# Joining row scans of layer 1 into 256 columns, and preparing two inputs a phase earlier

## The chip, the core and the metric

The kernel runs on one core of a Trainium2 chip. The metric is the time of one execution on the device, in microseconds, as the median of several runs. The engines are TensorE (PE; its weight loads are listed as PEld), VectorE (DVE), ScalarE (ACT), GpSimd (POOL) and SyncE (SP), which does nothing here but issue DMAs. ACT and POOL issue a few DMAs too.

## What is computed

The input `x` has 32 images of 48 channels, 64 rows and 128 columns, in float32. There are two layers. Each normalises its input by groups of channels, passes a convolution along one axis through the image row by row and then column by column, and adds its input:

```python
def step(w, b):
    def f(carry, inp):
        nxt = inp + _conv1d(carry, w, b)      # 48 x 48 channels, 5 taps
        return (nxt, nxt)
    return f
...
_, d_rest = jax.lax.scan(step(down_w, down_b), xs[0], xs[1:])      # 64 rows, downwards
...
_, u_rest = jax.lax.scan(step(down_w, down_b), u0, seq)            # 64 rows, upwards, the same weights
...
_, r_rest = jax.lax.scan(step(right_w, right_b), ws[0], ws[1:])    # 128 columns, to the right
...
_, l_rest = jax.lax.scan(step(left_w, left_b), l0, R[Ww - 2::-1])  # 128 columns, to the left
...
x = x + _L0_conv_ref(_gn(x), ...)
x = x + _L1_conv_ref(_gn(x), ...)
```

Each step of a scan needs the step before it. Different images are independent of each other.

## The kernel before

**Groups and phases.** The 32 images are four groups (0 to 3) of `GB` = 8. A row scan handles one group at a time: one row of one group is 128 columns (16 places along the image's width, beside 8 images) on three tiles of 128 partitions that hold 8 x 48 pairs of place and channel. A column scan handles two groups at a time, a pair. `PHASES` (line 103) lists the order of the work; "rows 1,2" means the row scans of layer 1 for group 2, "cols 0,0" the column scans of layer 0 for pair 0. A row phase is 63 steps down and 63 up, a column phase 127 right and 127 left.

**A step.** `step` (line 881) runs the nine products of `PRODUCTS` into three PSUM tiles of 128 columns, one for each of the three tiles of a row, and as each is complete VectorE adds the bias and the input to it and writes the new row or column into SBUF in place (line 903). Each product is two matmul instructions. Two of the nine have 96 weight columns and 120 moving columns, one has 112 weight columns. The order of the products is such that the first product of the next step needs the tile that was completed first. `row_step` and `col_step` call it; `scans` (line 955) yields all steps of a phase one after the other.

**Memory.** A group's 64 rows lie in two of the three `slot`s of the arena, 32 rows in each (`row_views`, line 688). Even phases use slots 0 and 1, odd phases 2 and 1 (`slots`, line 326). Column phases go through the image's width in four quarters, `quarter(k, j)`, one slot each.

**The order written out by hand.** Time is counted in steps. `at(t, fn)` puts work on an agenda, and before each step everything that is due is emitted (`catch_up`, line 1377). `in_order` (line 292) keeps that order on every engine, so each engine, and SyncE's queue of DMAs with it, takes its work strictly as the agenda lists it; an instruction that has to wait holds up all that stand behind it on its engine. An engine isn't held back to the agenda's time, though: it runs ahead as far as its data lets it.

- `plan_rows` (line 1006) loads a group's rows in blocks of 16 (`move_rows` from layer 0's rearranged input, `take_rows` from layer 1's input), has ACT scale them (`scale_rows`, 24 instructions a block), and stores the rows of the up scan in blocks of 8 (`move_rows` to DRAM, 10 DMAs each). Where a column phase follows directly, the last 8 rows go straight from the row layout into the column layout: `send_row` and `send_rest`, about 47 DMAs on each of the queues of SyncE and ACT.
- `plan_cols` (line 1054) loads the quarters, adds the residual on GpSimd, stores the result, and in layer 0 takes the statistics for layer 1 on VectorE and ACT.
- `plan_input` (line 986) prepares one group of the input in six parts: `take_in` fetches a part into a buffer (`nats`), GpSimd rearranges it (`permute`, 16 copies), four DMAs put it out (`put_out`), and ACT takes its statistics (`take_others`). `spread` then emits the small computation of scale and offset, one piece in each step. Group 1 has four buffers; groups 2 and 3 have one.

Layer 0's statistics of group 2 were prepared in cols 0,0, those of group 3 half in rows 0,2 and half in rows 1,0.

`last` is a buffer for the last row of the down scan, which the last step of the up scan adds.

Of the kernel before, what the change touches and what calls it, by code (L numbers as in the profile page):

```python
# [41 lines left out]
GB = 8  # L42
# [35 lines left out]
def weight_runs():  # L78
# [38 lines left out]


@with_exitstack
def kernel(  # L120
# [567 lines left out]
    def row_views(k):  # L688
        return [slot[i].rearrange("p (o h n) -> p o h n", o=NG, h=HALF) for i in slots(k)]

    def row(k, h):
        return row_views(k)[h // HALF][:, :, h % HALF]

    def move_rows(k, h0, h1, to_dram, q=None):

        _, layer, g = PHASES[k]
        view = row_views(k)[h0 // HALF]
        t = (ups if to_dram else source)[layer][g]
        for h in range(h0, h1, E8):
            end = min(h1, h + E8)  # L700
            for o in range(NG):
                for e, c0, c1, p0 in pieces(o):
                    here = view[p0 : p0 + c1 - c0, o, h % HALF : h % HALF + end - h]
# [12 lines left out]

    def take_rows(k, h0, h1, o):

        _, layer, g = PHASES[k]
        view = row_views(k)[h0 // HALF]  # L720
        for e, c0, c1, p0 in pieces(o):
            here = view[p0 : p0 + c1 - c0, o, h0 % HALF : h0 % HALF + h1 - h0]
            for q in range(NQ):
                dma(
                    here[:, :, q * RUN : (q + 1) * RUN],
                    by_quarter(source[layer][g], e, h0, h1, q)[c0:c1],
                )

    def scale_rows(k, h0, h1, groups=range(NG)):
        _, layer, g = PHASES[k]  # L730
        scale, offset = coeffs[layer, g]
        view = row_views(k)[h0 // HALF][:, :, h0 % HALF : h0 % HALF + h1 - h0]
        view = view.rearrange("p o h (k b) -> p o b h k", b=GB)
        for o in groups:
            for b in range(GB):
                args = view[:, o, b], scale[:, o, b : b + 1], offset[:, o, b : b + 1]
                nc.scalar.activation(  # L737
                    args[0], args[0], AF.Identity, bias=args[2], scale=args[1]
                )

    def scale_at_once(k, h0, h1, eng, o0=0, o1=NG):

        _, layer, g = PHASES[k]
        view = row_views(k)[h0 // HALF][:, o0:o1, h0 % HALF : h0 % HALF + h1 - h0]
        view = view.rearrange("p o h (k b) -> p o (h k) b", b=GB)
        for t, op in zip(coeffs[layer, g], (ALU.mult, ALU.add)):
            t = t[:, o0:o1].unsqueeze(2).to_broadcast([FULL, o1 - o0, (h1 - h0) * NK, GB])
            eng.tensor_tensor(view, view, t, op)
# [132 lines left out]
    def step(key, weights, b_at, src, inp, dst, whole, part):  # L881


        ps = [
            ps_step.tile([FULL, N], F32, tag=f"step{o}", name=f"step{o}_{key}")
            for o in range(NG)
        ]
        left = [sum(1 for p in PRODUCTS if p[1] == o) for o in range(NG)]
        seen = [0] * NG
        for i, o, s in PRODUCTS:  # L890
            seen[o] += 1
            m = COLUMNS.get((i, o, s), FULL)
            at = FULL * (o - NG * s - i + 1)
            nc.tensor.matmul(  # L894
                part(whole(ps[o])[0:m], -s),
                weights[:, i, at : at + m],
                part(src(i), s),
                start=seen[o] == 1,
                stop=seen[o] == left[o],
            )  # L900
            if seen[o] == left[o]:
                layer, way = b_at
                nc.vector.scalar_tensor_tensor(  # L903
                    dst(o),
                    whole(ps[o]),
                    bd[:, o, layer, way : way + 1],
                    inp(o),
                    ALU.add,
                    ALU.add,
                )  # L910

    def row_step(k, h, prev, inp, name):
        _, layer, g = PHASES[k]

        def part(t, s):
            return t[:, max(0, s) * GB : N + min(0, s) * GB]

        step(
            f"{layer}{g}{name}{h}",
            wt[f"down{layer}"],  # L920
            (layer, DOWN),
            lambda i: prev[:, i],
            lambda o: inp[:, o],
            lambda o: row(k, h)[:, o],
            lambda ps: ps,
            part,
        )

    def col_step(k, way, v0, v1):
# [10 lines left out]
        def part(t, s):  # L940
# [7 lines left out]
            col(v0),  # L948
            col(v1),
            col(v1),  # L950
            lambda ps: ps.rearrange("p (m b) -> p m b", b=GB),
            part,
        )

    def scans(k):
        if PHASES[k][0] == "rows":
            for h in range(1, H):
                yield lambda h=h: row_step(k, h, row(k, h - 1), row(k, h), "d")
            end = last.rearrange("p (o n) -> p o n", o=NG)
            for h in range(H - 2, -1, -1):  # L960
                yield lambda h=h: row_step(
                    k, h, row(k, h + 1), row(k, h - 1) if h else end, "u"
                )
        else:
            for v in range(1, W):
                yield lambda v=v: col_step(k, RIGHT, v - 1, v)
            for v in range(W - 2, -1, -1):
                yield lambda v=v: col_step(k, LEFT, v + 1, v)


    agenda = []
# [14 lines left out]
    def plan_input(g, times, work, lag, nats, perms):  # L986
# [5 lines left out]
        for j, t in enumerate(times):  # L992
# [11 lines left out]
        spread(t + work + lag + (0, 2, 32, 5)[g], scaling(f"x{g}", 0, g, stats, x_masks, (0, 0, 8, 0)[g]), 1)  # L1004

    def plan_rows(k, t0, prev):
        if k == 1:
# [5 lines left out]
        if k:  # L1013
            for i in range(4):
                if PHASES[k][1]:
                    for o in range(NG):
# [8 lines left out]
        seam = following and follows(k + 1)  # L1025
        if seam:
            cuts = cuts[2:]
            end = t0 + 2 * (H - 1)
# [4 lines left out]
            for q in range(1, NQ):  # L1033
                at(end + 0.1 if q == 1 else end + 1.6, move_rows, k, 0, 2 * E8, True, q)
        for h0, h1 in zip(cuts, cuts[1:]):
            t = t0 + 2 * (H - 1) - h0
            if k == 0:
                t += 16 if h0 >= HALF else 68
            elif not following:
                t = t0 + 92 + 5 * (H - h1) / E8 + (34 if h1 <= HALF else 0)  # L1040
            at(t, move_rows, k, h0, h1, True)
        at(
            t0 + H - 1,
            nc.gpsimd.tensor_copy,
            last.rearrange("p (o n) -> p o n", o=NG),
            row(k, H - 1),
# [7 lines left out]
    def plan_cols(k, t0, prev):  # L1054
# [5 lines left out]
        for i in range(n):  # L1060
# [3 lines left out]
                at(t0 - 13 + i, load_unit, k, 0, i, 2, 4, 0, E8, other)  # L1064
                at(t0 - 6 + i / n, load_unit, k, 0, i, 1, 2, 0, E8, other)
            else:
                early = 30 if after else 46 if k == 2 else 70
# [17 lines left out]
        for n_done, j in enumerate((3, 2, 1, 0)):  # L1085
            first, every = left + 34 + 32 * n_done, 4.5
            if j == 0 and PHASES[k + 1 if not final else k][0] == "rows":
                first, every = (end + 29, 6) if pair else (first, 7)
            units += [(first + every * i, j, i) for i in range(n)]
        stats = None  # L1090
        if layer == 0:
# [62 lines left out]
            store_result(k, 0, i, perm)  # L1154


    starts = [0]
    for kind, *_ in PHASES:
        starts.append(starts[-1] + 2 * ((H if kind == "rows" else W) - 1))
# [24 lines left out]
    at(starts[7] + 50, more_weights, "right", 1, RIGHT)  # L1184
    at(starts[7] + 54, more_weights, "left", 1, LEFT)


    def first_group():
# [191 lines left out]
            in_order(fn, *args)  # L1380

    for k in range(len(PHASES)):
        for one in scans(k):
            catch_up(done)
            in_order(one)
            done += 1
    catch_up(float("inf"))


# [51 lines left out]
```

## Time and profile before

| What | Value |
|---|---|
| Timed, median of 3 | 4165.44 us (4165.31 to 4170.69) |
| Profiled execution, its span from first to last instruction | 4158.1 us (the page gives no other time of it) |
| Mean granted TensorE clock | 0.989 |
| First step of the first scan | 60.7 us |
| DMA | 681.08 MB, mean 164 GB/s; 2008656 of 2208479 packets under 512 B |

The page lists for each engine the busy time, its share of the span and its instructions, then the span in 40 equal slices, the DMA queues, and the costliest groups of instructions. A group's row reads: line, engine, operation, what it writes and reads, shape, count, then busy time in us and mean of one in ns, then the idle time before it and what ended that. A row of stretches reads: the stretch, its length, for each engine its busy time and count of instructions, the granted clock, the DMA engines' share and GB/s. A row of the timeline reads: start, length, engine, line, operation, and in brackets the idle time before it and its releaser. SPq is SyncE's queue: each row there is a run of DMAs as they were issued, not as they landed.

The tiles of a step are named by layer and group or pair and direction: `step_01u` is rows 0,1 upwards, `step_00r` is cols 0,0 to the right. The scans of the phases start at (first matmul, us): rows 0,1 at 323.12, cols 0,0 at 577.40, rows 0,2 at 1081.07, rows 1,0 at 1344.66, rows 0,3 at 1596.38, cols 0,1 at 1850.34, rows 1,1 at 2351.51, rows 1,2 at 2608.13, rows 1,3 at 2857.88, cols 1,0 at 3107.59, cols 1,1 at 3604.21; the last matmul starts at 4101.85.

### The profile page before, as it was taken

The numbers are of one execution on the slowest core, as the hardware profiler recorded it, in microseconds if no ns is written. First come the engines' busy times: TensorE is split into PE (matmuls) and PEld (weight loads), VectorE is DVE, ScalarE is ACT, GpSimd is POOL, SyncE is SP. The second block draws the span as 40 slices with busy tenths as digits, with TensorE's granted clock in tenths as the row PEclk, the third lists the DMA queues.
The fourth block names the chain that finished last, engine by engine and source line by source line (L and its number), as shares of the span: only waits on it lengthen the run. The fifth ranks groups of instructions, "written<-read, shape, count | busy, mean of one in ns | idle before, by whom it ended". The sixth has DMA issues, their size and how long they took to land. (4 is left out here: it accounts for less than half of the span.)

```text
span 4158.1 us, 90227 instructions
## 1 busy us (share of the span) xinstructions
PE 4049.2 (97%) x36724; PEld 4031.7 (97%) x36724; DVE 2141.6 (52%) x6503; ACT 1251.6 (30%) x2440; POOL 826.1 (20%) x763
## 2 busy tenths in 40 slices
PE   6999999999999999999999999999999999999994
PEld 5999999999999999999999999999999999999994
DVE  6454444456654454444457664444444444444444
ACT  4645000536964543000006863423000002200122
POOL 5630010334222000010013220000000015610353
PEclk9999999999999999999999999999999999999997
DMA  9987769669979999258419979959289029999799
GB/s 299 229 184 121 116 127 214 209 159 252 218 188 163 173 163 156 35 103 194 107 30 273 181 147 145 141 93 150 49 141 208 1 55 247 295 257 155 146 233 197
DMA packets 2208479, 681.08 MB, mean 164 GB/s; under 512 B 2008656, under 2 KB 2157376, under 8 KB 2183488
## 3 DMA queue, kind: packets, MB, share of 16 engines
q1 hardware_dynamic: 2063936, 582.35, 68.4%
q10 hardware_dynamic: 141568, 87.46, 8.8%
q0 software_dynamic: 2560, 5.51, 0.5%
q8 instruction: 289, 4.73, 0.5%
q14 instruction: 126, 1.03, 0.1%
HBM read 398.29 MB, written 295.14 MB: 167 GB/s over the span
## 5 line engine op out<-in xcount | busy, mean ns | idle before, releaser
L829 POOL TENSOR_TENSOR arena<-arena 128x2048 f32<-128x2048 f32 x80 | 362.7, 4545 | 1481.7 <-PE step_10l L894 458.3
L737 ACT ACTIVATE arena<-arena,offset,scale 128x256 f32<-128x256 f32 (+2 forms) x744 | 538.4, 818 | 384.4 <-DMA arena<-mid 206.1
L674 POOL COPY arena<-arena 128x256 f32<-128x256 f32 x340 | 201.0, 659 | 447.6 <-DMA arena<-in_x 418.2
L612 ACT ACTIVATE early<-arena 128x256 f32<-128x256 f32 x192 | 129.7, 675 | 443.0 <-DMA arena<-xin 308.1
L894 PE MATMUL step_00r<-arena,early 128*128 128x128 f32 x2286 | 252.1, 274 | 6.1 <-DMA arena<-arena 5.1
L894 PEld LDWEIGHTS step_00r<-arena,early 128*128 128x128 f32 x2286 | 251.2, 185 | 7.0 <-issue 5.5
L894 PE MATMUL step_01r<-arena,early 128*128 128x128 f32 x2286 | 252.2, 274 | 5.8 <-DMA arena<-arena 4.9
L894 PEld LDWEIGHTS step_01r<-arena,early 128*128 128x128 f32 x2286 | 251.3, 185 | 6.6 <-issue 5.3
L894 PE MATMUL step_11r<-arena,early 128*128 128x128 f32 x2286 | 249.3, 272 | 0.3 <-DVE arena L903 0.3
L894 PEld LDWEIGHTS step_11r<-arena,early 128*128 128x128 f32 x2286 | 248.7, 184 | 0.8 <-DVE arena L903 0.7
L894 PE MATMUL step_00l<-arena,wleft 128*128 128x128 f32 x2286 | 249.2, 272 | 0.0
L894 PEld LDWEIGHTS step_00l<-arena,wleft 128*128 128x128 f32 x2286 | 248.7, 184 | 0.0
L894 PE MATMUL step_10l<-arena,wleft 128*128 128x128 f32 x2286 | 248.5, 272 | 0.0
L894 PE MATMUL step_11l<-arena,wleft 128*128 128x128 f32 x2286 | 248.5, 272 | 0.0
L894 PE MATMUL step_10r<-arena,early 128*128 128x128 f32 x2286 | 248.4, 272 | 0.0
L894 PE MATMUL step_01l<-arena,wleft 128*128 128x128 f32 x2286 | 248.4, 272 | 0.0
L894 PEld LDWEIGHTS step_10l<-arena,wleft 128*128 128x128 f32 x2286 | 248.4, 184 | 0.0
L894 PEld LDWEIGHTS step_11l<-arena,wleft 128*128 128x128 f32 x2286 | 248.4, 184 | 0.0
L894 PEld LDWEIGHTS step_01l<-arena,wleft 128*128 128x128 f32 x2286 | 248.4, 184 | 0.0
L894 PEld LDWEIGHTS step_10r<-arena,early 128*128 128x128 f32 x2286 | 248.4, 184 | 0.0
L297 ACT COPY early<-arena 128x1 f32<-128x1 f32 x2 | 0.4, 192 | 709.9 <-DVE arena L903 709.9
L851 ACT COPY arena<-arena 128x256 f32<-128x256 f32 x172 | 99.6, 656 | 362.4 <-POOL arena L829 256.3
(202 smaller groups left out, 7088.5 us busy)
## 6 DMA issues: line engine op xcount, KB each, us to landing
xin<-arena SPq DMA_DIRECT2D x94, 512.0 KB, 4.3
arena<-in_x SPq DMA_DIRECT2D x18, 2048.0 KB, 11.4
arena<-xin SPq DMA_DIRECT2D x96, 384.0 KB, 10.9
arena<-mid SPq DMA_DIRECT2D x384, 96.0 KB, 3.1
upb<-arena SPq DMA_DIRECT2D x192, 192.0 KB, 3.9
arena<-upb SPq DMA_DIRECT2D x96, 384.0 KB, 11.8
arena<-xin SPq DMA_DIRECT2D x174, 192.0 KB, 4.3
mid<-arena SPq DMA_DIRECT2D x32, 1024.0 KB, 11.2
```

The lines of the kernel that those rows point to most:

```text
L297: fn(*args)
L612: nc.scalar.activation(junk[:, 0:n], view[:, b], AF.Identity, accum_out=self.sum[:, i, j : j + 1])
L674: copy(dst[:, r, q], src[:, r0 + r, q])
L737: nc.scalar.activation(args[0], args[0], AF.Identity, bias=args[2], scale=args[1])
L829: eng.tensor_tensor(unit, unit, nat, ALU.add)
L851: copy(by_w(perm)[:, a], src[:, a])
L894: nc.tensor.matmul(part(whole(ps[o])[0:m], -s), weights[:, i, at : at + m], part(src(i), s), start=seen[o] == 1, stop=seen[o] == left[o],)
```

## The change

1. **Order.** "rows 1,0" moves behind "cols 0,1", so that all four row phases of layer 1 stand together.
2. **Joined scans.** Phases 8 and 9 (rows 1,2 and rows 1,3) are `JOINED`: the down scan of each runs together with the up scan of the group before it. `two_row_step` runs one step of both groups as 256 columns, with the same weights, into PSUM tiles of twice the width; VectorE's add covers both halves in one instruction, except in the last step, where it takes two.
3. **Places.** Since a joined group's rows come in while those of the group before go out, in the same slot, rows are loaded in blocks of 8 into the place of the block that has just been stored. `place` and `rows_at` work out where; `plan_rows` loads each block 34 steps ahead and scales it 17 steps ahead, counted in old steps, two for each joined one.
4. **Inputs.** Input 3 of 4 (group 2) is prepared in rows 0,1 instead of cols 0,0, one part each 9.5 steps instead of 13.5; input 4 (group 3) in cols 0,0 at the times that input 3 had.
5. **Small moves.** The residuals of the last quarter of cols 0,0 come later (from `end + 29`, every 6 steps, as those of cols 0,1 do already); the weights for layer 1's columns and the loads of cols 1,0 are moved with the phases.

```diff
@@ PHASES
     ("rows", 0, 2),
-    ("rows", 1, 0),
     ("rows", 0, 3),
     ("cols", 0, 1),
+    ("rows", 1, 0),
     ("rows", 1, 1),
...
+JOINED = (8, 9)
...
+    def place(k, h):
+        first = k
+        while first in JOINED:
+            first -= 1
+        since = k - first
+        turned = (since + 1) // 2 % 2 if h < HALF else since % 2
+        c = h % HALF // E8
+        return HALF // E8 - 1 - c if turned else c
...
-            ps_step.tile([FULL, N], F32, tag=f"step{o}", name=f"step{o}_{key}")
+            ps_step.tile([FULL, 2 * N], F32, tag=f"step{o}", name=f"step{o}_{key}")
...
+    def beside(a, b):
+        shift = b.offset - a.offset
+        assert a.ap == b.ap and shift > 0
+        return bass.AP(a.tensor, a.offset, [a.ap[0], (shift, 2), *a.ap[1:]])
+
+    def two_row_step(ku, hu, kd, hd):
...
+        step(
+            f"{layer}{g}u{hu}d{hd}",
+            wt[f"down{layer}"],
+            (layer, DOWN),
+            lambda i: both(row(ku, hu + 1), row(kd, hd - 1), i),
+            inp,
+            lambda o: both(row(ku, hu), row(kd, hd), o),
+            lambda ps: ps.rearrange("p (c n) -> p c n", c=2),
             part,
         )
...
+            if k not in JOINED:
+                for h in range(1, H):
+                    yield 1, lambda h=h: row_step(k, h, row(k, h - 1), row(k, h), "d")
...
+                if k + 1 in JOINED:
+                    yield 2, lambda h=h: two_row_step(k, h, k + 1, H - 1 - h)
...
+        if k in JOINED:
+            for i in range(H // E8):
+                h, t = i * E8, t0 + 2 * i * E8
+                for o in range(NG):
+                    at(t - 34 + 2 * o, take_rows, k, h, h + E8, o)
+                at(t - 17, scale_rows, k, h, h + E8)
...
+            elif up == 2:
+                t += 1
...
-                first, every = (end + 29, 6) if pair else (first, 7)
+                first, every = end + 29, 6
...
-    times = [starts[2] + 60 + 13.5 * j for j in range(6)]
-    plan_input(2, times, 6, 6, nats, tiles[2:4])
-    times = [t + 15 * j for t in (starts[3] + 42, starts[4] + 24) for j in range(3)]
-    plan_input(3, times, 6, 7, nats, tiles[2:4])
+    times = [starts[1] + 24 + 9.5 * j for j in range(6)]
+    plan_input(2, times, 6, 6, nats, tiles[2:4])
+    times = [starts[2] + 60 + 13.5 * j for j in range(6)]
+    plan_input(3, times, 6, 6, nats, tiles[2:4])
```

More of the change, by code (lines that the diff above doesn't have):

```diff
@@ L719, in take_rows @@
         _, layer, g = PHASES[k]
-        view = row_views(k)[h0 // HALF]
+        turned = h1 - h0 > E8 and place(k, h0) > place(k, h0 + E8)
+        if turned:
+            for h in range(h0, h1, E8):
+                take_rows(k, h, h + E8, o)
+            return
+        view = rows_at(k, h0, h1)
         for e, c0, c1, p0 in pieces(o):
-            here = view[p0 : p0 + c1 - c0, o, h0 % HALF : h0 % HALF + h1 - h0]
+            here = view[p0 : p0 + c1 - c0, o]
             for q in range(NQ):
@@ L902, in step @@
                 layer, way = b_at
[L903 to L910, printed above, removed]
+                to, sums, term = dst(o), whole(ps[o]), inp(o)
+                todo = [(to, sums, term)]
+                if isinstance(term, tuple):
+                    todo = [(to[:, c], sums[:, c], term[c]) for c in range(len(term))]
+                for to, sums, term in todo:
+                    nc.vector.scalar_tensor_tensor(
+                        to, sums, bd[:, o, layer, way : way + 1], term, ALU.add, ALU.add
+                    )
     def row_step(k, h, prev, inp, name):
@@ L924, in row_step, with both, inp, part @@
             lambda o: row(k, h)[:, o],
-            lambda ps: ps,
+            lambda ps: ps[:, 0:N],
+            part,
+        )
+    def beside(a, b):
[3 more added lines that the diff above has]
+    def two_row_step(ku, hu, kd, hd):
+        _, layer, g = PHASES[ku]
+        first = slots(ku)[0] < slots(kd)[0]
+        def both(u, d, o):
+            return beside(*((u[:, o], d[:, o]) if first else (d[:, o], u[:, o])))
+        def inp(o):
+            if hu:
+                return both(row(ku, hu - 1), row(kd, hd), o)
+            pair = last.rearrange("p (o n) -> p o n", o=NG)[:, o], row(kd, hd)[:, o]
+            return pair if first else pair[::-1]
+        def part(t, s):
+            return t[:, :, max(0, s) * GB : N + min(0, s) * GB]
+        step(
[6 more added lines that the diff above has]
+            lambda ps: ps.rearrange("p (c n) -> p c n", c=2),
             part,
@@ L1027, in plan_rows @@
             cuts = cuts[2:]
[L1028 removed]
+            end = t_up + up * (H - 1)
             at(end - E8, move_rows, k, E8, 2 * E8, True, 0)
@@ L1154, in last_results @@
             store_result(k, 0, i, perm)
-    starts = [0]
-    for kind, *_ in PHASES:
-        starts.append(starts[-1] + 2 * ((H if kind == "rows" else W) - 1))
+    starts, end = [], 0
+    for k, (kind, *_) in enumerate(PHASES):
+        n = (H if kind == "rows" else W) - 1
+        starts.append(end - 2 * n if k in JOINED else end)
+        end = starts[-1] + (2 if k in JOINED else 1) * n + (2 if k + 1 in JOINED else 1) * n
     for k, (kind, layer, _) in enumerate(PHASES):
@@ L1382 @@
     for k in range(len(PHASES)):
-        for one in scans(k):
+        for units, one in scans(k):
             catch_up(done)
             in_order(one)
-            done += 1
+            done += units
     catch_up(float("inf"))
```

49 lines of the change are left out of this document (27 added, 22 removed).

## The prediction

> **What bounds the kernel now.** First the page's first lines, then the busy time of each engine by stretches, one stretch for each of the five last row scans in layer 1.
>
> ```profile
> span 4158.1 us, 90227 instructions
> PE 4049.2 (97%) x36724; PEld 4031.7 (97%) x36724; DVE 2141.6 (52%) x6503; ACT 1251.6 (30%) x2440; POOL 826.1 (20%) x763
> ...
> 2477.00:2608.13 131.13, 131.13 (x1196) 131.13 (x1195) 66.47 (x231) 48.14 (x70) 3.88 (x13) 1.00 0.83 137
> 2608.13:2733.43 125.30, 125.28 (x1137) 124.80 (x1135) 61.07 (x190) 64.10 (x85) 1.42 (x6) 1.00 0.83 130
> 2733.43:2857.88 124.45, 124.45 (x1136) 124.45 (x1135) 60.67 (x189) 34.49 (x46) 0.50 (x1) 1.00 0.69 109
> 2857.88:2983.13 125.25, 125.25 (x1136) 124.80 (x1135) 60.87 (x189) 1.87 (x3) 0.00 (x0) 1.00 0.55 95
> 2983.13:3107.59 124.46, 124.46 (x1137) 124.46 (x1136) 60.66 (x189) 0.00 (x0) 0.51 (x1) 1.00 0.70 117
> ```
>
> TensorE never rests: a scan of 63 steps takes 124.45 us, 1.975 us a step, and a step is 9 products of 2 matmul instructions each (63 x 18 = 1134 of the about 1136 in the row), 109.7 ns apiece. VectorE is half idle. So time is gained only where a step gets cheaper, or where TensorE stands still. The first row is 6.7 us longer since it holds 60 more matmuls (statistics). I count time in these steps: step t of the second row phase (rows 0,1) lies at 323.1 + 1.975 t us, because that phase's 126 steps end at 572.3 (577.40 less 5.13, in the long fence of part 3).
>
> The sum is made in this execution (span 4158.1). The timed median is 4165.44, 7.3 us more, which lies around the span; I apply the differences to the median.
>
> **Part 1: joined scans.** Two up scans and two down scans, 4 x 63 steps of 128 columns, become 2 x 63 steps of 256. The trace has no 256-column matmul. It has 512-column ones, back to back, in the prologue (busy time in a stretch, that line's instructions alone), and rows for VectorE's add:
>
> ```profile
> 25.23:38.11 12.88, 12.88 (x32) 5.70 (x30) 1.00 1.02 418
> ...
> L903 DVE SCALAR_TENSOR_TENSOR arena<-step_11u,bd,arena 128x128 f32<-128x128 f32 x186 | 59.4, 347 | 63.6 <-PE step_11u L894 63.1
> L748 DVE TENSOR_TENSOR arena<-arena,offset 128x256 f32<-128x256 f32 x6 | 4.4, 741 | 0.2
> ```
>
> 30 of them start in 12.88 us: 429 ns each, 0.838 ns a column at most. 128 columns at that rate would take 107 ns; the step's mean is 109.7. So columns set nearly all of the spacing already. A 256-column matmul costs between 214.5 (half of 429) and 219.4 ns (twice 109.7); I take 216, near the 512 row. Four of 18 instructions have 240 columns: 203. One joined step is 14 x 216 + 4 x 203 = 3.836 us against 2 x 1.975 = 3.950. Times 126: **-14.4 us**; bounds 0 (no gain) and -18 (214.5 and 201).
>
> The Trainium skill ("TensorE: Matmul & The Clock Gate", section "Back-to-back issue gap") gives a sustained spacing of about 81 ns at 128 columns and 131 at 512; read as a straight line, 256 columns would be 98 ns, 1.2 times one step instead of 1.94, an estimate of -196 us for this part. The rows disagree: 429 against 109.7 is a factor of 3.9, not 1.6.
>
> VectorE's add on 256 columns isn't shown; between 347 ns and the 741 of an operation on 256 with a broadcast operand. A group's last product ends 8 instructions (1.7 us) before its sum is needed, so either end is hidden, and three of 0.74 a step are 2.2 of 3.8 us. The small hitches at a down scan's blocks (125.30 - 124.45 = 0.85 us) stay: 0.
>
> **SyncE in the joined stretch.** Loads now come by 8 rows, so twice as many DMAs: 40 loads and 10 stores in each 8 joined steps, 30.7 us.
>
> ```profile
> 2585.88 47.98 SPq L286 DMA_DIRECT2D arena<-mid  x80
> 2633.96 41.19 SPq L286 DMA_DIRECT2D upb<-arena  x40
> ```
>
> A 16-row load holds the queue 0.60 us, a store 1.03. Half as large, a load is between the 0.52 of tiny weight DMAs (13.00 us for 25, the row at 388.10 in part 3) and 0.60: 31.1 to 34.3 us for a turn of 30.7. That is tight, but loads are planned 34 old steps (65 us) ahead of the row; scaling's 15 us (24 at about 0.6) and the loads' own 22 leave some 28. At 0.52 the 13 turns fall 5 us behind: hidden, 0. At 0.60 they fall 47 behind: 19 us of stalls. I take 0, the nearer to the tiny DMAs, and keep +19 as a rival.
>
> **Part 2: phase order and layer 0's statistics.** Without input work in the third row phase (rows 0,2), and with the last residuals of cols 0,0 later, ACT's scaling of its last rows is no longer late:
>
> ```profile
> 1081.00:1215.00 134.00, 129.06 (x1151) 128.85 (x1150) 77.58 (x242) 113.02 (x223) 37.87 (x23) 0.97 0.93 210
> 2351.50:2477.00 125.50, 125.40 (x1136) 124.81 (x1135) 73.20 (x212) 97.49 (x183) 29.25 (x8) 1.00 0.86 163
> ...
> 1163.03 17.87 ACT L737 ACTIVATE arena<-arena,offset,scale 128x256 f32<-128x256 f32 x24 [6.21 <-issue]
> ...
> 1181.38 2.00 PE L894 MATMUL step_02d<-arena,early 128*128 128x128 f32 x8 [4.94 <-issue]
> ```
>
> TensorE waited 4.94 us, until the scaling ended at 1180.9 (and the mean clock of the stretch is 0.97). The second row is the down scan after cols 0,1, which already has the late residuals: 125.5. Difference 8.5, of which 1.3 are statistics that only move (12 matmuls): **-7 us** (0 to -8.5).
>
> **Part 3: input 3 (index 2) goes into phase rows 0,1.** This is the step that decides. SyncE's queue in that phase today:
>
> ```profile
> 326.64 42.25 SPq L286 DMA_DIRECT2D arena<-xin  x40
> 368.94 6.44 SPq L286 DMA_DIRECT2D wleft<-in_mask  x10
> 375.47 9.24 SPq L286 DMA_DIRECT2D upa<-arena  x10
> 384.75 3.18 SPq L286 DMA_DIRECT2D taps<-in_w  x5
> 388.10 13.00 SPq L286 DMA_DIRECT2D early<-taps  x25
> 401.21 9.98 SPq L286 DMA_DIRECT2D upa<-arena  x10
> 411.24 3.95 SPq L286 DMA_DIRECT2D taps<-in_w  x5
> 415.35 12.35 SPq L286 DMA_DIRECT2D wleft<-taps  x25
> 427.80 42.59 SPq L286 DMA_DIRECT2D upa<-arena  x30
> ...
> 486.86 3.43 SPq L286 DMA_DIRECT2D arena<-upa  x7
> 492.80 16.20 SPq L286 DMA_DIRECT2D upa<-arena  x10
> 509.10 1.61 SPq L286 DMA_DIRECT2D arena<-upa  x3
> 510.81 50.11 SPq L286 DMA_DIRECT2D upa<-arena  x40
> 561.02 32.51 SPq L286 DMA_DIRECT2D arena<-arena  x47
> ...
> 577.40 0.77 PE L894 MATMUL step_00r<-arena,early 128*128 128x128 f32 x2 [5.13 <-DMA arena<-arena]
> ```
>
> One queue, strictly in program order. Today it runs ahead of the scan until it catches up with TensorE: the loads planned at step 80 (481 us) go at 486.9. Then come the last stores, each waiting for its rows, and at 561.0 the sends of the last 8 rows into the column layout. TensorE stands from 572.3 to 577.4 for these: first half of the sends, 16.4 us after 561.0. So every microsecond by which the sends start later stalls TensorE.
>
> What one buffer of input costs is seen where the work is done today, in cols 0,0 (SyncE's queue, GpSimd, and the engines in that stretch; last a DMA group's median time to landing):
>
> ```profile
> 764.45 0.37 SPq L286 DMA_DIRECT2D arena<-in_x  x1
> 774.72 7.46 SPq L286 DMA_DIRECT2D xin<-arena  x4
> 785.29 0.37 SPq L286 DMA_DIRECT2D arena<-in_x  x1
> ...
> 772.27 9.53 POOL L674 COPY arena<-arena 128x256 f32<-128x256 f32 x16 [11.37 <-DMA arena<-in_x]
> ...
> 764.40:785.30 20.90, 20.90 (x195) 20.90 (x194) 10.32 (x32) 12.56 (x34) 9.53 (x16) 1.00 0.59 202
> ...
> arena<-in_x SPq DMA_DIRECT2D x18, 2048.0 KB, 11.4
> ```
>
> Fetch 7.8 us, GpSimd's permutation 9.5, ACT's statistics 13.0 beside it; the next fetch waits for ACT (one buffer): 20.8 us at best, and the change plans one each 9.5 steps, 18.8 us. Each of the 4 put-outs waits for its permutation **at the head of SyncE's queue**, and so do all stores, weights and loads behind it. Followed through in queue order, with 9 us a landing (between 7.8 and 11.4), 9.9 a store of 10:
>
> ```profile
> 364.55 17.95 ACT L737 ACTIVATE arena<-arena,offset,scale 128x256 f32<-128x256 f32 x24 [3.62 <-issue]
> ```
>
> - Fetch 1 at 368.9, behind the 40 loads. Landed 378, ACT done 391: fetch 2 at 391.
> - ACT's order puts this 17.95 us scaling between statistics 1 and 2: scaled at 409 (needed at step 48, 417.9: hidden, 9 us to spare), statistics 2 done 422: fetch 3 at 422.
> - One store, then the wait: fetch 4 at 444. Weights, store, weights, two put-outs (46 us): fetch 5 at 491. Two stores and put-outs: fetch 6 at 518. The same: the loads of step 80 go at 545 instead of 486.9.
> - Their unhidden rest: loads and a store 22.2 (486.86 to 509.10), again 15.4 (to about 524.5), then stores of 10 to 15, 10 and 5 us. Sends at about 610 instead of 561.
>
> **+49 us** at the seam; +25 with landings of 7.8, stores of 8 and cheap put-outs, +62 with landings of 11.4. Everything after the seam is planned relative to it and moves along. Input 4 takes input 3's old place in cols 0,0, so nothing new there.
>
> **Sum.** -14.4 - 7 + 49 = +27.6, that is 4193; its own range is 4169 to 4207 (25 and 62 at the seam).
>
> **The rivals.**
> - *The preparation fits* (faster): SyncE reaches the sends before step 119 although it waits, because waits and stores overlap more than I follow. It needs the 58 us of delay at step 80 to shrink below the slack, 13 us. For: there is some room, since the 30 stores from 427.80 take 42.6 us where 30 at 1.03 would take 31. Against: the order in the queue. Then -14.4 - 7 = 4144. Chance 0.25.
> - *SyncE also loses the joined stretch* (slower still): decides at more than 0.55 us a load; +19 at 0.60: 4212, up to 4235 at 0.65. Chance 0.14.
> - *Doubling columns buys nothing* (the change doesn't do what it says): a joined step costs 3.95. 4165.4 - 7 + 49 = 4207. For: 109.7 is close to 107. Chance 0.07.
> - *Columns are nearly free*, the weight loads set the spacing (PEld is as busy as PE): a joined step costs between 1.975 and 2.4 us. For: the skill's rule above. Against: 429. At 2.4, -196 - 7 + 49 = 4012. Chance 0.01.
>
> My forecast has 0.53. About 0.2% (8 us) is what a measurement here can tell from no change: below 4157, only the first and last rival, 0.26; within, a half-hidden seam, 0.11; above, 0.63. The range 4141 to 4222 takes in the first rival and half of the second.
>
> **What would show it.** Right: TensorE idle for 40 to 60 us before the first col step of cols 0,0, released by a DMA; SyncE's queue waiting on POOL and ACT between 376 and 545. Joined scans of 241.7 us each, with no wait for ACT's scaling or for loads; the down scan of rows 0,2 at about 125.5. Wrong: a seam of about 5 us, or joined matmuls of another spacing than 216 ns.

## The result and the profile after

| | us | ratio to before, 95% interval |
|---|---|---|
| before, median | 4166.71 | |
| forecast | 4193 (4141 to 4222) | |
| changed kernel, median | 4373.41 (4368.05 to 4376.26) | 1.0486 [1.0472, 1.05] |
| changed kernel, profiled span | 4371.1 (before 4158.1) | |

The change costs 5%: 213.0 us between the two spans, where the forecast had 27.6. First the page's first lines of the changed kernel, then its busy time in four stretches: the down scan of rows 0,2, the two joined scans, and the gap before cols 0,0.

```profile
span 4371.1 us, 86080 instructions
...
PE 4063.2 (93%) x34456; PEld 3962.1 (91%) x34456; DVE 2071.2 (47%) x6119; ACT 1303.0 (30%) x2632; POOL 829.9 (19%) x775
```

```profile
1158.00:1282.50 124.50, 124.50 (x1137) 124.50 (x1136) 72.83 (x213) 100.38 (x190) 28.28 (x7) 1.00 0.89 182
2550.30:2871.60 321.30, 256.60 (x1136) 215.23 (x1134) 88.99 (x193) 85.91 (x169) 1.01 (x2) 0.92 0.48 77
2871.60:3194.50 322.90, 259.49 (x1134) 216.56 (x1135) 88.45 (x190) 81.54 (x160) 0.00 (x0) 0.89 0.40 64
574.70:652.70 78.00, 0.41 (x4) 0.22 (x3) 0.59 (x2) 0.00 (x0) 16.31 (x34) 0.53 0.91 155
```

TensorE, 97% busy before, now has two places where it stands. The joined scans take 321.3 and 322.9 us where 63 x 3.83 = 241.3 were expected: 161 us too much, at a mean clock of 0.92 and 0.89. The gap before cols 0,0 is 78 us, forecast at 54: 24 us too much. 161 + 24 = 185 is the whole of what the forecast missed (213.0 - 27.6). The down scan of rows 0,2 is 124.5 us, as hoped.

**Inside a joined scan.** Timeline of the changed kernel around the eighth to tenth joined step (start, length, engine, operation, count, and in brackets the idle time before it and its releaser):

```profile
2576.17 8.98 SPq L287 DMA_DIRECT2D upb<-arena  x10
2577.15 4.00 PE L917 MATMUL step_11u55d<-arena,early 128*128 128x256 f32 x18
2580.75 12.26 ACT L760 ACTIVATE arena<-arena,offset,scale 128x128 f32<-128x128 f32 x24 [31.32 <-PE step_11u55d L917]
2581.18 0.48 DVE L931 SCALAR_TENSOR_TENSOR arena<-step_11u55d,bd,arena 128x256 f32<-128x256 f32 x1 [0.77 <-PE step_11u55d L917]
2585.19 20.29 SPq L287 DMA_DIRECT2D arena<-mid  x40
...
2588.99 5.69 PEld L917 LDWEIGHTS step_11u54d<-arena,early 128*128 128x128 f32 x18 [8.25 <-ACT arena L760]
2588.99 6.09 PE L917 MATMUL step_11u54d<-arena,early 128*128 128x256 f32 x18 [7.84 <-DMA arena<-mid]
2594.91 4.00 PE L917 MATMUL step_11u53d<-arena,early 128*128 128x256 f32 x18
```

ACT scales a block of rows that no step needs yet. It starts only about when the step of 2577.15 ends: that step released it, after 31 us of idling. The next step starts only when two thirds of the 24 scalings are done. TensorE loses 8.0 us (from start to start 11.84 instead of 3.83). The granted clock drops while it stands, and the step after the stall, at a mean clock of 0.66, takes 5.92 us instead of 3.83: another 2.1.

```profile
2588.99:2594.91 5.92, 5.92 (x18) 4.76 (x19) 0.87 (x2) 4.02 (x8) 0.00 (x0) 0.66 0.49 78
```

The two joined scans have fourteen such stalls, of 7.8 to 12.3 us each, three of them in two pieces (the expectations below speak of sixteen). TensorE is idle for 128 us in these scans (644.2 less the 516.1 in which it is busy); the other 33 of the 161 us are the steps at the lower clock. SyncE is not late: 10 stores and 40 loads are 29.3 us in a turn of 30.7, 0.51 us a load.

**At the seam.** SyncE's queue of the changed kernel, from the 40 row loads over the third and later fetches of input 3 to the sends, then TensorE's first column step:

```profile
330.60 42.44 SPq L287 DMA_DIRECT2D arena<-xin  x40
...
426.64 0.37 SPq L287 DMA_DIRECT2D arena<-in_x  x1
427.10 15.65 SPq L287 DMA_DIRECT2D upa<-arena  x10
...
470.10 10.00 SPq L287 DMA_DIRECT2D upa<-arena  x10
...
500.67 1.32 SPq L287 DMA_DIRECT2D arena<-in_x  x1
502.09 18.22 SPq L287 DMA_DIRECT2D upa<-arena  x10
...
521.65 12.25 SPq L287 DMA_DIRECT2D upa<-arena  x10
...
535.24 1.20 SPq L287 DMA_DIRECT2D arena<-in_x  x1
536.53 16.79 SPq L287 DMA_DIRECT2D upa<-arena  x10
...
554.62 12.33 SPq L287 DMA_DIRECT2D upa<-arena  x10
...
568.31 4.85 SPq L287 DMA_DIRECT2D arena<-upa  x7
...
636.36 31.83 SPq L287 DMA_DIRECT2D arena<-arena  x47
```

```profile
652.73 7.48 PE L917 MATMUL step_00r<-arena,early 128*128 128x128 f32 x44 [77.62 <-DMA arena<-arena]
```

The column loads go at 568.3 (before 486.86, forecast 545), the sends 68 us behind them (before 74, forecast 65), and TensorE waits for the sends. Five of the six runs of ten stores ahead of the column loads took 12 to 18 us; the sixth, at 470.10, with no fetch or put-out right before it, took 10.0. The forecast had 9.9 for each, from rows of the kernel before (9.24 and 9.98). SyncE also waited for GpSimd's permutation and for ACT's statistics, 41.5 us in all in 320 to 640 us (in total, times, longest):

```profile
SPq L287 <- POOL arena L675: 24.2, 14, 10.0
SPq L287 <- ACT early L536: 17.3, 3, 12.8
```

### The profile page after: what moved, and what is told of

The parts are those of the page before. It is cut to its first block, busy times and chain, and to the rows that moved or that the text cites. A ratio compares the mean times of both kernels' runs of the same rounds, so it can differ in the third digit from the quotient of the medians.

```text
span 4371.1 us, 86080 instructions
## 1 busy us (share of the span) xinstructions
PE 4063.2 (93%) x34456; PEld 3962.1 (91%) x34456; DVE 2071.2 (47%) x6119; ACT 1303.0 (30%) x2632; POOL 829.9 (19%) x775
## 5 line engine op out<-in xcount | busy, mean ns | idle before, releaser
L760 ACT ACTIVATE arena<-arena,offset,scale 128x256 f32<-128x256 f32 (+2 forms) x936 | 589.8, 723 | 620.2 <-DVE arena L931 187.2
L917 PE MATMUL step_00r<-arena,early 128*128 128x128 f32 x2286 | 252.3, 274 | 78.4 <-DMA arena<-arena 77.6
L931 DVE SCALAR_TENSOR_TENSOR arena<-step_00r,bd,arena 128x128 f32<-128x128 f32 x381 | 122.1, 348 | 209.5 <-PE step_00r L917 126.3
```

What stands on the lines that cost most here:

```text
L760: nc.scalar.activation(args[0], args[0], AF.Identity, bias=args[2], scale=args[1])
L917: nc.tensor.matmul(part(whole(ps[o])[0:m], -s), weights[:, i, at : at + m], part(src(i), s), start=seen[o] == 1, stop=seen[o] == left[o],)
L931: nc.vector.scalar_tensor_tensor(to, sums, bd[:, o, layer, way : way + 1], term, ALU.add, ALU.add)
```

## The experiments

Twelve kernels ran, each timed four times or more, with the kernel before beside them; each ratio is to the kernel before as it was timed beside that run (medians of 4166.71 to 4168.45).

| Run | us, median | ratio to before, 95% interval | seam: idle before the first column step |
|---|---|---|---|
| before | 4166.71 | | 5.1 |
| changed | 4373.41 | 1.0486 [1.0472, 1.05] | 77.6 |
| e1_apart | 4229.12 | 1.0147 [1.0132, 1.0162] | 75.3 |
| e2_split_dve | 4362.73 | 1.0467 [1.0451, 1.0483] | 77.4 |
| e3_queues | 4367.39 | 1.0479 [1.0464, 1.0495] | 71.6 |
| e4_nojoin | 4227.14 | 1.0142 [1.0125, 1.0159] | 79.2 |
| e5_carry | 4221.13 | 1.0132 [1.0118, 1.0146] | 76.9 |
| e6_nowait | 4207.26 | 1.0097 [1.0083, 1.011] | 50.8 |
| e7_split_prep | 4225.71 | 1.0141 [1.0126, 1.0156] | 53.8 |
| e8_old_join1 | 4165.58 | 0.9996 [0.9986, 1.0007] | 6.1 |
| e9_nofetch | 4175.12 | 1.0011 [1.0001, 1.0021] | 20.6 |
| e10_lateput | 4180.31 | 1.0028 [1.0017, 1.004] | 20.5 |
| e11_old_join1_ends | 4162.54 | 0.9983 [0.9974, 0.9991] | 5.6 |
| e12_old_join1_units | 4172.39 | 1.001 [1.0, 1.002] | 6.8 |

### What stalls the joined steps

Theory A: `beside` describes two rows in two slots with one operand, a stride from slot to slot. The program derives from such operands which instruction must wait for which; it takes this one as touching everything between its two rows, and thus the blocks that ACT scales and DMAs load and store. Theory B: SyncE's queue is late.

**e1_apart**: the phases stay joined, with all loads, places and scalings where they are, but each joined step is two steps of 128 columns.

```diff
-                    yield 2, lambda h=h: two_row_step(k, h, k + 1, H - 1 - h)
+                    yield 2, lambda h=h: apart(k, h, k + 1, H - 1 - h, end)
...
+    def apart(ku, hu, kd, hd, end):
+        row_step(ku, hu, row(ku, hu + 1), row(ku, hu - 1) if hu else end, "u")
+        row_step(kd, hd, row(kd, hd - 1), row(kd, hd), "d")
```

> Joined phases with the same loads, scaling, stores and places, but each joined step run as two steps of 128 columns, one after the other, so that no operand spans two rows. Theory A (the operand that spans two rows is ordered as if it covered all that lies between them, so that each block's scaling and loads, written between two steps, must end before the next step): the waits of 8 to 14 us every 8 steps vanish; the joined stretch takes 126 x 3.95 = 498 us instead of 644; time about 4229. Theory B (SyncE is late, since the loads of 8 rows are twice as many): the waits stay, and the steps cost 0.12 us more: 4373 to 4390. The seam's 78 us stay in both.

4229.12. The busy time of its whole joined stretch:

```profile
2550.70:3050.30 499.60, 499.37 (x4507) 496.56 (x4507) 241.81 (x752) 171.60 (x328) 0.51 (x1) 1.00 0.57 91
```

499.6 us with TensorE busy for 499.4, beside 644 in the changed kernel. The loads, the stores and the scalings are the same: SyncE and ACT keep up. Theory B falls.

**e2_split_dve**: only VectorE's add is split into two adds of one row each; the matmul keeps the two-row operand.

```diff
-                todo = [(to[:, c], sums[:, c], term[c]) for c in range(len(term))]
+                todo = [(to[c], sums[:, c], term[c]) for c in range(len(term))]
...
-            lambda o: both(row(ku, hu), row(kd, hd), o),
+            lambda o: pair_of(row(ku, hu), row(kd, hd), o),
```

> Only VectorE's add is split into two adds of 128 columns with operands of single rows; TensorE's matmuls keep the 256-column operand over two rows. Theory A: TensorE's read alone is enough to order the scaling against the step, so most of the wait stays: 4330 to 4380. If the waits come from VectorE's in-place write alone: about 4215. Theory B: 4373.

4362.73: the stall stays. The same turn as above in this kernel's timeline:

```profile
2576.41 4.00 PE L917 MATMUL step_11u55d<-arena,early 128*128 128x256 f32 x18
2588.26 6.58 PE L917 MATMUL step_11u54d<-arena,early 128*128 128x256 f32 x18 [7.85 <-ACT arena L760]
```

TensorE's reading of the two rows is enough. What was left open is whether the operand or the 256 columns do it.

**e5_carry**: 256-column matmuls as in the change, but the operand is a compact buffer in which the two rows lie side by side (two such buffers, in turns). VectorE writes both halves there, and GpSimd copies the rows back.

```diff
-            lambda i: both(row(ku, hu + 1), row(kd, hd - 1), i),
-            inp,
-            lambda o: both(row(ku, hu), row(kd, hd), o),
+            lambda i: old[:, i],
+            lambda o: (up[:, o], down[:, o]),
+            lambda o: new[:, o],
...
+        nc.gpsimd.tensor_copy(row(ku, hu), new[:, :, 0])
+        nc.gpsimd.tensor_copy(down, new[:, :, 1])
```

> The changed kernel, in which the joined steps still run as 256 column matmuls, but the operand no longer spans two slots: the two rows of a step stand side by side in a small buffer (two copies of it, taken in turns), VectorE writes the sums there in two halves, and GpSimd copies both rows back to their places (two copies a step). Theory A (the two row operand, a stride from one slot to another, is ordered as if it touched everything between its rows, so that the scaling of later blocks waits for a step and holds up the next): the 16 stalls of 8 to 14 us go, the joined stretch takes about 484 us instead of 644, and the kernel about 4373 - 161 = 4212 us. Rival W (256 column matmuls as such run into the stall, by their width or by the granted clock): the stretch stays near 644 us and the kernel near 4373. Rival G (GpSimd's copies, about 1 us a step of 3.84 us, hold a step up): between, above 4230.

4221.13. Its two joined scans by busy time:

```profile
2556.40:2801.00 244.60, 243.35 (x1134) 208.09 (x1134) 110.85 (x378) 96.08 (x184) 60.35 (x126) 0.99 0.60 95
2801.00:3047.50 246.50, 243.35 (x1134) 207.96 (x1134) 110.76 (x378) 75.45 (x145) 62.18 (x130) 0.99 0.56 89
```

The same matmuls in 491 us instead of 644: the stalls are gone, GpSimd's copies (0.51 us each, 60 us a scan) hide. That settles it: the operand that spans two slots costs 153 us net, not the width. 484 were expected; the 7 us more lie mostly at the ends, where TensorE waits for GpSimd to fill the buffer ahead of each joined scan (below) and to copy the last rows back:

```profile
2556.45 3.84 PE L917 MATMUL step_11u62d<-arena,early 128*128 128x256 f32 x11 [1.97 <-POOL arena L959]
...
2802.73 3.50 PE L917 MATMUL step_12u62d<-arena,early 128*128 128x256 f32 x9 [2.94 <-POOL arena L959]
```

### What makes the seam so long

**e4_nojoin**: `JOINED = ()`, so the new order and the new times of the inputs alone.

> No scans joined: the new phase order and the new times of the inputs alone. All four row phases of layer 1 as before, 124.5 to 131 us a scan: 4373 - 145 = 4229 by theory A and B alike; against the kernel before +63: the seam (+72) less the stall in rows 0,2 (-8).

4227.14, with 79.2 us at the seam. The joined scans play no part there.

**e3_queues**: input 3's fetches go to ACT's queue and its put-outs to GpSimd's, away from SyncE (the joined steps as in the change).

```diff
-        dma(nat, src[:, :, r0 * W : (r0 + n) * W])
+        dma(nat, src[:, :, r0 * W : (r0 + n) * W], nc.scalar if g == 2 else None)
...
+                    nc.gpsimd if g == 2 else None,
```

> Input 3's fetches are issued from ACT's queue and its put-outs from GpSimd's, so that nothing of its preparation waits at the head of SyncE's queue. If the stall at the seam comes from SyncE's order (the prediction's part 3), it falls from 78 us to 5 to 15: 4300 to 4312. Rival: the DMA engines have no room for 25 MB more in that phase: the stall stays above 40, 4335 or more.

A miss: 4367.39, the seam still 71.6 us. What SyncE waited for longest in 320 to 640 us, and rows of its queue:

```profile
SPq L287 <- DMA arena<-in_x: 49.1, 4, 15.7
```

```profile
327.60 63.62 SPq L287 DMA_DIRECT2D arena<-xin  x40
...
460.03 24.32 SPq L287 DMA_DIRECT2D upa<-arena  x10
...
562.28 3.37 SPq L287 DMA_DIRECT2D arena<-upa  x7
```

SyncE no longer waits for GpSimd's permutation or ACT's statistics, but four times, 49.1 us in all, for fetches that it doesn't issue. Waits stand inside the rows shown: 15.2 us of the 63.6 of the 40 loads are the first of the four, 10.2 of the 24.3 of ten stores are for VectorE's rows. Without them the loads took 48.4 us (42.4 in the changed kernel) and the stores 14.1. Why SyncE waits for these fetches wasn't tried and stays open. So this run doesn't tell whether waiting at the head of the queue is the cause, and I asked how much of the loss is waiting at all.

**e6_nowait**: e4_nojoin with all DMAs of input 3, but without its permutation and statistics, so SyncE's queue doesn't wait for GpSimd or ACT there.

```diff
-                at(t + i * work / per, permute, nat, r, perm, [nc.gpsimd])
+                if g != 2:
+                    at(t + i * work / per, permute, nat, r, perm, [nc.gpsimd])
...
-            at(t + lag, stats.take_others, pieces_of * j, nat)
+            if g != 2:
+                at(t + lag, stats.take_others, pieces_of * j, nat)
```

> The changed kernel with the joined steps taken apart entirely (no joined phases, as in e4_nojoin), and for input 3 of the four the preparation keeps every DMA, its fetches and its put-outs, but leaves out GpSimd's permutation and the statistics (its sums are constants), so nothing in SyncE's queue waits for GpSimd or ACT there. Layer 0's second and third rows, and what comes from them, are computed from other numbers. Against e4_nojoin's 4227 us with 79.5 us lost at the seam. Theory O (in-order waits at the head of SyncE's queue make the column loads and the sends late): seam 20 us or less, the kernel 4165 to 4170. Theory C (the DMA engines' capacity: fetches, put-outs and weights together are more than the window holds, whoever waits): seam 40 us or more, the kernel at 4190 or above.

4207.26. SyncE's queue and TensorE's first column step:

```profile
509.67 17.25 SPq L287 DMA_DIRECT2D upa<-arena  x10
...
541.86 4.67 SPq L287 DMA_DIRECT2D arena<-upa  x7
```

```profile
627.40 14.15 PE L917 MATMUL step_00r<-arena,early 128*128 128x128 f32 x108 [50.83 <-DMA arena<-arena]
```

Without the waits for GpSimd and ACT the seam is 28 us shorter (79.2 - 50.8). 46 us over the 5 of before remain: the transfers cost that much even so, and ten stores right behind a fetch still take 17 us, in the row at 509.67 without a wait for anything. That is theory C's side of the test. The two parts can't simply be added, though: the waits in the changed kernel were 41.5 us long, and with them gone the same transfers follow each other more closely (205 GB/s instead of 180, below).

**e9_nofetch and e10_lateput** take e6_nowait apart: the first leaves out the six fetches, the second sends the 24 put-outs 255 steps later.

```diff
-            if j + ahead < len(times):
+            if j + ahead < len(times) and g != 2:
...
-                at(t + i * work / per + 4, put_out, g, rows * j + r, perm)
+                at(t + i * work / per + (255 if g == 2 else 4), put_out, g, rows * j + r, perm)
```

> e6_nowait (no joined steps, no permutation and no statistics of input 3) without the six fetches of input 3 of 2 MB each; its 24 put-outs of 512 KB stay, so layer 0's third row group is computed from other numbers. e6_nowait lost 51.1 us at the seam. If that is the DMA engines' time (theory C: six fetches at 10.6 us from issue to landing are some 60 us of it), the seam falls to 25 us or less. If it is SyncE's own time to issue (24 put-outs at 0.86 us against six fetches at 1.1 us), the fetches are the smaller part and the seam stays at 38 us or more.

> e6_nowait with the fetches in their place and input 3's 24 put-outs sent 255 steps later, in the second half of the column phase, behind the seam (what they store is not input 3). Theory C: the put-outs are the other part of the DMA engines' time, the seam falls to 25 us or less; SyncE's issue time: down to 51 - 21 = 30 us. If the two parts each take more than half the seam away, they compete for one thing that had room for one of them. The column phase may then lose time of its own; only the seam is read.

Both seams fell below 25 us, as theory C had it, and not as SyncE's own time to issue would have it. First e9_nofetch, then e10_lateput, SyncE's queue and the first column step:

```profile
480.35 12.12 SPq L287 DMA_DIRECT2D upa<-arena  x10
...
507.58 4.83 SPq L287 DMA_DIRECT2D arena<-upa  x7
```

```profile
594.62 17.38 PE L917 MATMUL step_00r<-arena,early 128*128 128x128 f32 x126 [20.62 <-DMA arena<-arena]
```

```profile
511.39 3.32 SPq L287 DMA_DIRECT2D arena<-upa  x7
```

```profile
596.19 13.86 PE L917 MATMUL step_00r<-arena,early 128*128 128x128 f32 x108 [20.49 <-DMA arena<-arena]
```

Six fetches take SyncE about 1 us each to issue, yet without them the seam is 30 us shorter. The column loads go 34 us earlier without them: 6 are the fetches' own issue, 14 are stores that take less, the rest is in weights, put-outs and waits. Ten stores took 17 us behind a fetch with both kinds of transfers, 12 to 13.6 with put-outs alone, 12.4 to 15.1 with fetches alone, 9.0 to 10 with neither near them. Either kind alone costs 15 us over the 5 of before, both together 46. What lengthens an issue inside stays open. On average the DMA engines were not full. From 373 to 563 us, in the kernel before, the changed one and e6_nowait (DMA share and GB/s stand last):

```profile
373.00:563.00 190.00, 190.00 (x1735) 190.00 (x1734) 92.49 (x289) 9.50 (x13) 15.40 (x32) 1.00 0.71 120
```

```profile
373.00:563.00 190.00, 190.00 (x1734) 190.00 (x1734) 92.65 (x290) 92.91 (x222) 61.89 (x107) 1.00 0.71 180
```

```profile
373.00:563.00 190.00, 190.00 (x1734) 190.00 (x1733) 92.53 (x289) 14.77 (x20) 5.07 (x11) 1.00 0.85 205
```

The average hides two stretches of e6_nowait. In the first, where weights are loaded, ten stores took 9.75 us; in the second, with the engines full, 12 to 17:

```profile
433.00:473.00 40.00, 40.00 (x367) 40.00 (x366) 19.23 (x60) 0.00 (x0) 0.51 (x1) 1.00 0.37 64
473.00:563.00 90.00, 90.00 (x822) 90.00 (x822) 44.08 (x138) 0.00 (x0) 0.00 (x0) 1.00 1.00 218
```

So busy DMA engines are the nearest candidate. It isn't shown: in the kernel before their share was 0.89 in 473 to 563 us, and the 40 stores from 510.81 on took 10.1 us for ten there, without the 9.8 us that they waited for VectorE.

**e7_split_prep**: e5_carry with two of input 3's six parts behind the seam, and input 4 following them. In this kernel the shifted parts come to share buffers with the column phase's work, which changes some of layer 0's values.

> e5_carry with input 3's preparation cut in two: its first four parts in the second row phase at 14 steps apart, the last two behind the seam, 24 and 36 steps into the column phase, and input 4's parts follow from 72 steps on at 13 steps apart. If the seam's loss comes from what is queued ahead of the column loads and the sends (theories O and C both say so), the seam goes back to 5 to 15 us and the kernel to 4212 - 65 = 4147 us, up to 4160. Rival: the work moved behind the seam delays the first half of the column phase (its own loads and stores run there until step 66): 10 to 40 us come back as stalls inside the column scan, 4160 to 4190.

A miss: 4225.71, no better than e5_carry. The seam shrinks from 76.9 to 53.8 us, 23 less for two parts of six, about their share of the 72. But TensorE then stands in the first column scan:

```profile
762.14 6.68 PE L917 MATMUL step_00r<-arena,early 128*128 128x128 f32 x36 [27.44 <-DVE arena L931]
```

27.4 us come back there, within the 10 to 40 of the rival: the work only moved. The rival's time, 4160 to 4190, took the seam for cured, and it wasn't.

### Is there a version that gains?

**e8_old_join1** keeps the order and the input times of before and joins one pair, rows 1,2 and 1,3 (`JOINED = (9,)`), in e5_carry's form. The other pair can't be joined in that order, because by the agenda group 2's scale is not ready by then.

> The order of phases and the times of inputs 3 and 4 of the kernel before, with one joined stretch alone (the up scan of layer 1's third row phase with the fourth's down scan), in the form of e5_carry. A joined step took 3.83 us in the trace against 2 x 1.975: 63 x 0.12 = 7.4 us less than the kernel before, 4159 us. If the joined stretch stalls here too (loads and stores of both phases in half the time), 4166 or more.

4165.58, a ratio of 0.9996 [0.9986, 1.0007]: no difference that can be told. **e11_old_join1_ends** runs the first and last joined step as two single steps.

> e8_old_join1 with the first and the last of the 63 joined steps run as two single steps, which read and write the rows themselves, so that neither the fill of the small buffer (2.2 us of TensorE's time ahead of the stretch) nor the copy out of it (1.85 us behind) holds a step up. e8's span was 4155.7: 4152, against 4158 before; in the medians 4161 to 4163 against 4167. If the two stops have another cause they stay, 4165.

The down scan of rows 1,2 up to the up scan of rows 1,3, by busy time, in the kernel before, in e8 and in e11:

```profile
2608.10:2983.10 375.00, 374.98 (x3404) 374.04 (x3404) 182.61 (x568) 100.49 (x133) 1.92 (x7) 1.00 0.69 112
```

```profile
2608.50:2978.90 370.40, 367.00 (x2270) 331.69 (x2268) 172.07 (x569) 128.53 (x230) 63.33 (x135) 1.00 0.58 91
```

```profile
2622.30:2989.40 367.10, 367.08 (x2307) 333.21 (x2306) 172.13 (x568) 126.07 (x226) 61.27 (x131) 1.00 0.58 92
```

375.0, 370.4, 367.1: the 7 us of one joined pair are all there (7.9) once the ends no longer wait for GpSimd. The median is 4162.54, 0.9983 [0.9974, 0.9991] of before: the one version that beats the kernel before, by under 0.2%. The span of its profiled execution (4164.1) is above before's all the same: in that one the down scan of rows 0,2 stood for 8.8 us (4.9 before), and the scans around it lost more too.

**e12_old_join1_units** takes e11 and moves the result units of the last quarter of cols 0,0 later (20 steps behind the scan, 6 apart; they are six units, where the expectation says ten). They share buffers with input 4's parts, which changes some of layer 0's values here too.

```diff
-                first, every = (end + 29, 6) if pair else (first, 7)
+                first, every = (end + 29, 6) if pair else (end + 20, 6)
```

> e11_old_join1_ends, and the last column block of rows 0 and 1's column phase has its ten result units from 20 steps behind the scan on, 6 steps apart, where the kernel before began 3 steps behind it, 7 apart (the changed kernel 29, 6). If these units' loads and stores held up the third row phase (8.2 us lost there before, 0.2 in the changed kernel), about 6 us more go: span 4146, median 4156. If not, as e11; if the scales of layer 1's first row group become late by it, its down scan loses more than 1 us and the time rises.

A miss. TensorE in the down scan of rows 0,2, first in e11_old_join1_ends, then here:

```profile
1195.21 5.17 PE L917 MATMUL step_02d<-arena,early 128*128 128x128 f32 x23 [8.76 <-issue]
```

```profile
1201.44 3.95 PE L917 MATMUL step_02d<-arena,early 128*128 128x128 f32 x17 [18.53 <-DVE arena L931]
```

The stall grew to 18.5 us from 8.8. Later units alone don't cure it; beside input 4's preparation they make it worse.

## Why the prediction was wrong, step by step

- **Spacing of 256 columns: right.** 3.83 us a step from start to start, 3.836 forecast; part 1's mechanism is worth the 7 us a pair that e11 shows. The Trainium skill ("TensorE: Matmul & The Clock Gate", section "Back-to-back issue gap") would have had some 98 ns a matmul by the straight line through its figures; 3.83 us for 18 are 213 ns, so this trace doesn't bear it out.
- **VectorE's add hidden, SyncE's loads at 0.52 us: right.** 0.48 us an add, 0.51 us a load; the rival that SyncE loses the joined stretch fell with e1_apart. By the prediction's own working 0.65 us a load would have given it 4238 rather than 4235, and 62 us at the seam 4206 rather than 4207; neither matters.
- **"Joined scans of 241.7 us each, with no wait for ACT's scaling or for loads": wrong, 161 us.** This is the step that failed. The forecast priced the engines and the queue in the joined stretch, and never asked what the new two-row operand would be ordered against: its sum has the waits for ACT's scaling and for loads at 0. No rival had them either; the slowest of them ended at 4235. What the runs showed instead: fourteen stalls, 128 us of idle and 33 at a lower clock. The four scans' -14.4 became +147. e5_carry against the changed kernel shows the cause, 153 us of it gone with the operand alone.
- **Part 2, -7: right in size.** 124.5 us against 134.0, of which 1.3 are statistics that moved. Which of its two reasons carries it is not settled; e12 speaks against the later residuals alone.
- **Part 3, +49: right place, wrong size.** It became +72 (77.6 - 5.1 = 72.5), beyond the upper bound of 62. The column loads went 23 us later than forecast (568.3 against 545). The term that was mis-sized most is the price of ten stores beside the fetches, taken as 9.9 us: 18.22, 12.25, 16.79 and 12.33 are 20 us more than four times that, of which put-outs that were cheaper than forecast gave 6 back. (The 15.65 at 427.10 cost nothing: SyncE had to wait for ACT behind it anyway.) Another 4 us were there from the start, since the 40 row loads went at 330.6 instead of 326.6, and 5 came where SyncE waited on its way through the weights. The rest behind the column loads was nearly right (68 against 65). The reason given, waits at the head of the queue, holds in part: without them 28 us go (e6_nowait), and 46 stay with the traffic, which the forecast counted at nearly nothing. How the traffic lengthens an issue is open.
- **The sum** was 27.6. With 161 for the stalls and 24 at the seam it is 213, the measured difference of the spans.

## What to carry to other kernels

Before joining two pieces of work into one instruction, look at what its operands span, not only at how long it takes: a strided operand over two buffers was ordered against all that lay between them, and a small buffer with the rows side by side gave the gain back. DMAs that are added to a queue cost more than their own issue: measure how long that queue's other DMAs take beside such transfers, and take that price. Work that is moved ahead of a seam is free only if the queue that the seam waits for has room; here its place before had been the better one.

## What was not expected of the hardware

- Ten stores of SyncE took 9.0 to 10.0 us to issue with no other kind of transfer near them, 12 to 13.6 beside put-outs of 512 KB (e9_nofetch), and 17 to 18 just behind a fetch of 2 MB with put-outs around it (e6_nowait), with at most 2.4 us of waiting for VectorE in a run of ten. Other queues didn't help: beside fetches on ACT's queue, 40 loads of SyncE took 48.4 us without the wait that stood among them, 42.4 in the changed kernel (e3_queues).
- A stall of 8 us costs TensorE two more: the step after it took 5.92 us instead of 3.83, at a granted clock of 0.66. Over the two scans, with seven such stalls in each, the mean clock was 0.92 and 0.89.
